# Edge scores of a graph network: rows of 256 columns, added, clipped and weighted, in place of maxima and minima of 257 scaled and sorted columns

## The chip, the cores and the metric

The kernel runs on one core of a Trainium2 chip. The metric is the device time of one execution in microseconds (us); lower is better. Three runs of the kernel before have a median of 3169.38 us, from 3156.57 to 3185.58. Everything is computed in 32-bit floats. The names used here: PE is TensorE (matrix products), DVE is VectorE, ACT is ScalarE, POOL is GpSimd, SP issues transfers.

## The reference, cut to what matters

A batch of 16 graphs with 1024 nodes and 256 features goes through four layers. All share one sparse adjacency matrix `adj` (about 1.6% of it is not zero).

```
# layer 0, for each graph b
pre_u = h @ W1[:256]                      # (1024, 256)
pre_v = h @ W1[256:]                      # (1024, 256)
S[u, v] = sigmoid( sum_k W2[k] * relu(pre_u[u, k] + pre_v[v, k] + b1[k]) + b2 )
a[v]  = sum_u S[u, v] * adj[u, v] * h[u]
m[v]  = (sum_u adj[u, v] * h[u]) * h[v]
z     = beta1*h + beta2*(a @ Wa + ba) + beta3*(m @ Wm + bm)
# layer 1
z     = z + relu((adj @ z) @ W.T + b)
# layers 2 and 3: attention over all pairs of nodes, with adj as a bias in the softmax
```

The change concerns `S`, the edge scores of layer 0. They are needed only where `adj[u, v]` is not zero. `relu(x)` is `max(x, 0)`.

## The kernel before, in words

**Edge lists.** At the start the kernel finds, for each node u, its neighbours v by repeated searches for the eight largest values of a row of `adj` (the loop over `t` in the preparation). The first 16 neighbours of each node go into the lists `slot_v`, the further ones into extra rows of four. 1024 nodes are 8 tiles of 128 nodes (a tile's nodes lie on the 128 partitions); six extra tiles follow. One **edge step** handles one tile and one neighbour slot, for four graphs at once. There are 4 groups of 4 graphs and (8 x 16 + 6 x 4) = 152 steps a group, 608 in all.

**Sides.** `edge_sides` computes for each graph and node the two projected rows and the product with Wa in one go (2 R + 256 columns, copied from PSUM by ScalarE into `st`), and stores them to DRAM as `u_d`, `v_d` and `hw_d`. R is the width of a row: 257 before. Four graphs lie side by side, so a row of a group is 4 R numbers wide.

**The trick with sorted columns.** For a positive weight w, `w * max(a + b, 0)` is `max(w a, -w b) + w b`; for a negative one the maximum becomes a minimum. So the preparation sorts the 256 columns by the sign of W2, scales the u side by W2 and the v side by -W2, and puts the sum of `w b` into one extra column in front. To this end it counts and ranks the signs with many tiny VectorE instructions (from `above` to `to_sign`), turns both halves of W1 by transposes on TensorE, multiplies them with placing matrices (`to_own`, `to_other`), and makes `b1r` and `sign` by products. The columns are cut at fixed places: the first 145 take a maximum (`BIG`, the extra one, 112 surely positive and 32 mixed), the last 112 a minimum, and the 32 mixed ones, where the sign changes, are scaled by their size only and multiplied by their sign afterwards. If the signs do not fit this cut, `uneven` sends the kernel into a slow arm that needs no lists.

**An edge step** (`score_steps`): GpSimd gathers 128 rows of `v_d` by an indirect transfer into one of six tiles z (`fetch`, five steps ahead, lines 1113-1115 through the helper at line 942). The tile u holds the node's own rows: ScalarE copies `b1r` into it (line 1105) and a transfer adds the rows of `u_d` to it (line 1109). Then come three VectorE instructions on z, in place:

```
big, low, mixed = zk[:, :, :BIG], zk[:, :, BIG:], zk[:, :, BIG - MIXED : BIG]
paced(nc.vector.tensor_tensor(big, big, uk[:, :, :BIG], ALU.max))      # line 1076, 4 x 145
paced(nc.vector.tensor_tensor(low, low, uk[:, :, BIG:], ALU.min))      # line 1077, 4 x 112
nc.vector.tensor_tensor(mixed, mixed, sign..., ALU.mult)               # line 1078, 4 x 32
```

One step later four ScalarE passes (line 1031) sum each graph's R columns of z into the score `s`. After a tile's last slot ScalarE applies a tanh, VectorE multiplies by `adj` (line 1036), and GpSimd scatters the values into a dense matrix in DRAM (line 947), from where they come back as `gd`.

**What sets the order.** Beside the edge steps runs the main work: first the products that need no scores (the messages m, the sides of the next graphs; `score_free`), then for each group the products with the dense scores (`with_edges`), layer 1 (`layer_one`, written as seven products of blocks instead of eight, `seven`), and two attention layers (`front`, `sums`). `Side.along` calls one edge step for a fixed amount of main work, by the table `PACE` (0.246 to 0.3 steps per written microsecond of TensorE work). So the 608 steps are interleaved with the main work in program order, on the same engines, and each engine works through its own queue in order. `paced` makes an instruction wait for the sixth TensorE product back in program order. Products are recorded at line 140, whichever function asks for them. In `sums` VectorE makes tiles m (line 1458), three ahead, and four products of TensorE use each. The scores of a group must be finished before its `with_edges`. A scheduler places the instructions of each engine by its own estimate of times, within the dependencies.

Steps and the main work share VectorE with the additions that put the seven products together (`put_together`, line 419), the copies `gc` of the dense scores (line 1490, every second one; the others on ScalarE at line 1492) and the closing additions of each attention layer.

Of the kernel before, what the change touches and what calls it, by code (L numbers as in the profile page):

```python
# [17 lines left out]
P = 128  # L18
# [25 lines left out]
MIXED = 32  # L44
LOW = 3.0e38
# [34 lines left out]
def gnn_stack_kernel(  # L80
# [41 lines left out]
    def bank():  # L122
        return psum[-1].tile([P, HN], F32, tag="bank", name="bank")
# [56 lines left out]
    def column(a, name, queue=nc.gpsimd):  # L180

        t = const.tile([P, DH], F32, name=name)
        queue.dma_start(t, a.rearrange("(h p) -> p h", p=P))
        return t
# [5 lines left out]

    SURE = (D - MIXED) // 2
    BIG = 1 + SURE + MIXED
    R = 1 + D
    b1r = const.tile([P, R], F32, name="b1r")
    sign = const.tile([P, MIXED], F32, name="sign")
# [307 lines left out]
    with ExitStack() as stack:  # L503
# [5 lines left out]
        def first_group():  # L509
# [13 lines left out]
        index = prep1.tile([P, DH], F32, name="index")  # L523
        nc.gpsimd.iota(
            index, pattern=[[P, DH]], base=0, channel_multiplier=1, allow_small_or_imprecise_dtypes=True
        )
        places = prep1.tile([P, D], F32, name="places")
        nc.gpsimd.iota(
            places, pattern=[[1, D]], base=0, channel_multiplier=0, allow_small_or_imprecise_dtypes=True
        )  # L530

        w2c = column(g0_W2.rearrange("d o -> (d o)"), "w2c", nc.sync)
        b1c = column(g0_b1, "b1c", nc.scalar)
# [9 lines left out]
        def tiny(name):  # L543
            return prep1.tile([P, DH], F32, name=name)

        above = tiny("above")
        nc.vector.tensor_scalar(above, w2c, 0.0, None, ALU.is_gt)
        counted = bank()
        nc.tensor.matmul(counted[:, :DH], below, above, start=True, stop=True)
        nc.tensor.matmul(counted[:, DH : 2 * DH], ones, above, start=True, stop=True)  # L550
        work = first_group()
        next(work)
        rank, n_above = tiny("rank"), prep1.tile([P, DH], F32, name="n_above")
        nc.vector.tensor_copy(n_above, counted[:, DH : 2 * DH])
        nc.vector.tensor_copy(rank, counted[:, :DH])
        nc.vector.tensor_scalar(rank[:, 1:], rank[:, 1:], n_above[:, 0:1], None, ALU.add)
        n_all = prep1.tile([P, 1], F32, name="n_all")
        nc.vector.tensor_tensor(n_all, n_above[:, 0:1], n_above[:, 1:2], ALU.add)
        others, place = tiny("others"), tiny("place")
        nc.vector.tensor_tensor(others, index, rank, ALU.subtract)  # L560
        nc.vector.scalar_tensor_tensor(others, others, n_all, rank, ALU.add, ALU.subtract)
        nc.vector.tensor_tensor(place, others, above, ALU.mult)
        nc.vector.tensor_tensor(place, others, place, ALU.subtract)
        nc.vector.tensor_tensor(place, place, rank, ALU.add)
        size, scale, back = tiny("size"), tiny("scale"), tiny("back")
        nc.vector.scalar_tensor_tensor(size, w2c, -1.0, w2c, ALU.mult, ALU.max)
        nc.vector.tensor_scalar(scale, place, float(SURE + MIXED), None, ALU.is_lt)
        nc.vector.tensor_tensor(size, size, w2c, ALU.subtract)
        nc.vector.tensor_tensor(size, size, scale, ALU.mult)
        nc.vector.tensor_tensor(scale, size, w2c, ALU.add)  # L570
        nc.vector.tensor_scalar(back, scale, -1.0, None, ALU.mult)
        signs = tiny("signs")
        nc.vector.tensor_scalar(signs, above, 2.0, -1.0, ALU.mult, ALU.add)
        to_own = prep1.tile([P, DH, R], F32, name="to_own")
        to_other = prep1.tile([P, DH, R], F32, name="to_other")
        to_sign = prep1.tile([P, DH, MIXED], F32, name="to_sign")
        nc.vector.memset(to_own[:, :, 0], 0.0)
        nc.vector.tensor_copy(to_other[:, :, 0], w2c)
        for kh in range(DH):
            for dst, by, at in (  # L580
                (to_own[:, kh, 1:], scale, slice(0, D)), (to_other[:, kh, 1:], back, slice(0, D)),
            ):
                placed = nc.vector.tensor_scalar(
                    dst, places[:, at], place[:, kh : kh + 1], by[:, kh : kh + 1], ALU.is_equal, ALU.mult
                )
        for kh in range(DH):
            late = nc.vector.tensor_scalar(
                to_sign[:, kh, :], places[:, SURE : SURE + MIXED], place[:, kh : kh + 1], signs[:, kh : kh + 1],
                ALU.is_equal, ALU.mult,
            )  # L590
            after(tc, late, [placed], mybir.DependencyClass.NoSync, "behind the weights")
        w1 = prep1.tile([P, DH, 2 * R + D], F32, name="w1p")
        turned_w = {}
        for side in range(2):
            ps = bank()
            for kh in range(DH):
                for dh in range(DH):
                    at = (kh * DH + dh) * P
                    nc.tensor.transpose(ps[:, at : at + P], raw[:, dh, side, kh * P : (kh + 1) * P], ident)
            turned_w[side] = prep1.tile([P, DH, DH * P], F32, name=f"turned_w{side}")  # L600
            nc.scalar.activation(turned_w[side], ps.rearrange("p (k d) -> p k d", k=DH), AF.Copy)
        for side, to_side in ((0, to_own), (1, to_other)):
            for dh in range(DH):
                ps = bank()
                for kh in range(DH):
                    nc.tensor.matmul(
                        ps[:, :R], turned_w[side][:, kh, dh * P : (dh + 1) * P], to_side[:, kh, :],
                        start=kh == 0, stop=kh == DH - 1,
                    )
                nc.scalar.activation(w1[:, dh, side * R : (side + 1) * R], ps[:, :R], AF.Copy)  # L610
        last_w = nc.vector.tensor_scalar(w1[:, :, 2 * R :], raw[:, :, 2, :], beta2, 0.5, ALU.mult, ALU.mult)
        nc.sync.dma_start(w_d, w1.rearrange("p c k -> p (c k)"))
        ps = bank()
        for kh in range(DH):
            nc.tensor.matmul(
                ps[:, :R], b1c[:, kh : kh + 1].to_broadcast([P, P]), to_own[:, kh, :],
                start=kh == 0, stop=kh == DH - 1,
            )
        nc.scalar.activation(b1r, ps[:, :R], AF.Copy)
        nc.vector.memset(b1r[:, 0:1], -LOW)  # L620
        ps = bank()
        for kh in range(DH):
            nc.tensor.matmul(ps[:, :MIXED], ones, to_sign[:, kh, :], start=kh == 0, stop=kh == DH - 1)
        nc.vector.tensor_copy(sign, ps[:, :MIXED])

        spare_row = prep1.tile([P, NF], F32, name="spare_row")
# [1403 lines left out]
```

## Time and profile before

One execution was profiled: 3179.84 us, of which 3178.1 us are the span from the first instruction to the last.

| what | busy us | share of the span |
|---|---|---|
| TensorE (PE) | 3034.1 | 95% |
| VectorE (DVE) | 2077.4 | 65% |
| ScalarE (ACT) | 1815.8 | 57% |
| GpSimd (POOL) | 1679.1 | 53% |

| group of instructions | count | mean ns |
|---|---|---|
| line 1031, ScalarE pass that sums 257 columns | 2432 | 410 |
| line 1031, reading its accumulator | 2432 | 193 |
| line 942, gather of 128 rows of 4 x 257 | 512 | 1139 |
| line 947, scatter of scores | 512 | 1118 |
| line 1458, tile m of the attention sums | 512 | 745 |

How to read it: busy times of an engine count each moment once, while the mean of a group is that of single instructions, which may overlap by some tens of ns at their ends. A row of groups gives the line, the engine, the operation, what is written and read, partitions x elements, the count, the busy time of the group with the mean of one, and the idle time of the engine just before them with what ended most of it. A line of waits reads "who <- whom: us in total, times, longest". In a matrix product, each of the two records counts as one instruction.

### The profile page before, as it was taken

The numbers are of one execution on the slowest core, as the hardware profiler recorded it, in microseconds if no ns is written. First come the engines' busy times: TensorE is split into PE (matmuls) and PEld (weight loads), VectorE is DVE, ScalarE is ACT, GpSimd is POOL, SyncE is SP. The second block draws the span as 40 slices with busy tenths as digits, with TensorE's granted clock in tenths as the row PEclk, the third lists the DMA queues.
The fourth block names the chain that finished last, engine by engine and source line by source line (L and its number), as shares of the span: only waits on it lengthen the run. The fifth ranks groups of instructions, "written<-read, shape, count | busy, mean of one in ns | idle before, by whom it ended". The sixth has DMA issues, their size and how long they took to land. (4 is left out here: it accounts for less than half of the span.)

```text
span 3178.1 us, 40600 instructions
## 1 busy us (share of the span) xinstructions
PE 3034.1 (95%) x11774; PEld 2158.6 (68%) x11774; DVE 2077.4 (65%) x4093; ACT 1815.8 (57%) x6461; POOL 1679.1 (53%) x1481
## 2 busy tenths in 40 slices
PE   8899999899998999999999899999999999989999
PEld 5445444444546855887785588878658888858888
DVE  8857565656574676777666677766767763258844
ACT  3326565566674866777676577867757762213342
POOL 1116566777563576555667764656665550077600
PEclk9999999999999999999999999999999999999999
DMA  8978997988999987558988755788875555485600
GB/s 290 321 281 294 311 286 244 299 258 238 287 266 338 309 261 240 149 157 248 304 272 260 228 159 154 244 302 279 271 224 160 155 162 169 146 273 167 165 7 28
DMA packets 314738, 731.46 MB, mean 230 GB/s; under 512 B 50493, under 2 KB 144762, under 8 KB 307338
## 3 DMA queue, kind: packets, MB, share of 16 engines
q0 software_dynamic: 128064, 388.90, 41.7%
q1 hardware_dynamic: 148234, 271.98, 26.0%
q10 hardware_dynamic: 38208, 67.91, 5.8%
q8 instruction: 95, 1.56, 0.2%
q14 instruction: 137, 1.12, 0.1%
HBM read 592.10 MB, written 136.53 MB: 229 GB/s over the span
## 5 line engine op out<-in xcount | busy, mean ns | idle before, releaser
L1031 ACT ACTIVATE z<-z 128x257 f32<-128x257 f32 x2432 | 985.1, 410 | 569.4 <-DVE z L1078 303.3
L140 PE MATMUL bank<-feats,m 128*128 128x257 f32 x4096 | 925.1, 384 | 26.8 <-DVE m L1458 15.6
L140 PEld LDWEIGHTS bank<-feats,m 128*128 128x128 f32 x4096 | 775.3, 192 | 147.6 <-DVE m L1458 17.9
L942 POOL DMA_INDIRECT z<-v_d,slot_v x512 | 583.1, 1139 | 541.8 <-ACT z L1031 278.8
L1076 DVE TENSOR_TENSOR z<-z,u 128x580 f32<-128x580 f32 x608 | 461.7, 759 | 427.1 <-PE bank L140 185.1
L947 POOL DMA_INDIRECT dense_d<-gt,slot_at x512 | 572.2, 1118 | 187.9 <-issue 142.0
L140 PE MATMUL bank<-gc,hw 128*128 128x256 f32 x2048 | 454.1, 383 | 27.5 <-ACT gc L1492 17.6
L1031 ACT ACTIVATION_READ_ACCUMULATOR z<-z 128x1 f32 x2432 | 468.3, 193 | 2.1 <-issue 2.1
L1458 DVE SCALAR_TENSOR_TENSOR m<-rho,tau,adj_sb 128x512 f32<-128x512 f32 x512 | 374.8, 745 | 140.4 <-PE bank L140 120.8
L140 PEld LDWEIGHTS bank<-gc,hw 128*128 128x128 f32 x2048 | 388.3, 191 | 92.8 <-ACT gc L1492 24.0
L1077 DVE TENSOR_TENSOR z<-z,u 128x448 f32<-128x448 f32 x608 | 375.8, 618 | 0.0
L140 PE MATMUL bank<-w1p,hT 128*128 128x385 f32 x1024 | 346.1, 491 | 11.7 <-issue 5.3
L140 PEld LDWEIGHTS bank<-w1p,hT 128*128 128x128 f32 x1024 | 193.8, 190 | 162.7 <-issue 30.1
L140 PE MATMUL bank<-g_wT,z 128*128 128x257 f32 x1024 | 233.4, 382 | 5.7 <-DVE t L419 2.7
L140 PE MATMUL bank<-adj_sb,h 128*128 128x512 f32 x504 | 224.6, 595 | 0.0
L140 PEld LDWEIGHTS bank<-g_wT,z 128*128 128x128 f32 x1024 | 192.8, 191 | 38.1 <-issue 4.7
L1492 ACT ACTIVATE gc<-gd 128x1024 f32<-128x1024 f32 x64 | 132.1, 2064 | 124.3 <-PE bank L140 93.3
L942 POOL DMA_INDIRECT z<-v_d,x_node x96 | 129.0, 1343 | 137.4 <-ACT z L1031 67.1
L369 ACT ACTIVATE st<-bank 128x385 f32<-128x385 f32 x256 | 121.6, 483 | 132.2 <-PE bank L140 78.9
L140 PEld LDWEIGHTS bank<-adj_sb,h 128*128 128x128 f32 x504 | 96.1, 191 | 115.9 <-issue 107.4
L1078 DVE TENSOR_TENSOR z<-z,sign 128x128 f32<-128x128 f32 x608 | 172.6, 284 | 0.0
L140 PE MATMUL bank<-adjT_in,t 128*128 128x512 f32 x352 | 155.2, 593 | 4.0 <-DMA adjT_in<-sumT_d 3.7
(248 smaller groups left out, 3245.7 us busy)
## 6 DMA issues: line engine op xcount, KB each, us to landing
gd<-dense_d SPq DMA_DIRECT2D x128, 512.0 KB
dense_d<-zero ACTq DMA_DIRECT2D x64, 512.0 KB
h<-in_x_dram SPq DMA_DIRECT2D x19, 1024.0 KB
u_d<-st SPq DMA_DIRECT2D x128, 128.5 KB
v_d<-st SPq DMA_DIRECT2D x128, 128.5 KB
u<-u_d POOLq DMA_DIRECT2D x32, 514.0 KB
hw_d<-st SPq DMA_DIRECT2D x128, 128.0 KB
zb_d<-zb ACTq DMA_DIRECT2D x16, 1024.0 KB
```

Of the source, the lines that this page charges most:

```text
L140: recent.append(nc.tensor.matmul(*args, **kw))
L369: nc.scalar.activation(st[:, cols], ps[:, :half], AF.Copy)
L942: return nc.gpsimd.indirect_dma_start(out=dst, out_offset=None, in_=src[:], in_offset=bass.IndirectOffsetOnAxis(ap=at, axis=0), **how,)
L947: return nc.gpsimd.indirect_dma_start(out=dst[:], out_offset=bass.IndirectOffsetOnAxis(ap=at, axis=0), in_=src, in_offset=None,)
L1031: nc.scalar.activation(zk[:, c, :], zk[:, c, :], AF.Copy, accum_out=s[:, k, c : c + 1])
L1076: paced(nc.vector.tensor_tensor(big, big, uk[:, :, :BIG], ALU.max))
L1077: paced(nc.vector.tensor_tensor(low, low, uk[:, :, BIG:], ALU.min))
L1078: nc.vector.tensor_tensor(mixed, mixed, sign[:, None, :].to_broadcast([P, GB, MIXED]), ALU.mult)
L1458: nc.vector.scalar_tensor_tensor(m, r[:, cols], ta[:, kt : kt + 1], ea[:, kt, cols], ALU.max, ALU.mult)
L1492: paced(nc.scalar.activation(gc, by_batch, AF.Copy), 16)
```

## The change

Rows are 256 columns wide. Neither side is scaled or sorted; there is no extra column, no sign, no cut. `b1r` and a new constant `w2r` are `b1` and `W2` themselves, read from DRAM into all partitions. A step adds u to z over all 4 x 256 numbers, and a second instruction takes the maximum with 0 and multiplies by `w2r`, which is repeated for the four graphs. The preparation uses W1 as it was loaded; only Wa is scaled by beta2 / 2 in place. Loads of `w2c` and `b1c`, which only the slow arm needs now, move from the SP and ScalarE queues to GpSimd's. Three waits ("behind the weights") that held back instructions of the preparation go, and so does the test `uneven`.

```diff
-    SURE = (D - MIXED) // 2
-    BIG = 1 + SURE + MIXED
-    R = 1 + D
-    b1r = const.tile([P, R], F32, name="b1r")
-    sign = const.tile([P, MIXED], F32, name="sign")
+    R = D
+    b1r = everywhere(g0_b1, D, "b1r")
+    w2r = everywhere(g0_W2.rearrange("d o -> (d o)"), D, "w2r")
...
-        w2c = column(g0_W2.rearrange("d o -> (d o)"), "w2c", nc.sync)
-        b1c = column(g0_b1, "b1c", nc.scalar)
+        w2c = column(g0_W2.rearrange("d o -> (d o)"), "w2c")
+        b1c = column(g0_b1, "b1c")
...
-        above = tiny("above")
-        nc.vector.tensor_scalar(above, w2c, 0.0, None, ALU.is_gt)
-        counted = bank()
-        nc.tensor.matmul(counted[:, :DH], below, above, start=True, stop=True)
...
+        w1 = raw.rearrange("p c s k -> p c (s k)")
+        nc.vector.tensor_scalar(w1[:, :, 2 * R :], w1[:, :, 2 * R :], beta2, 0.5, ALU.mult, ALU.mult)
+        nc.sync.dma_start(w_d, w1.rearrange("p c k -> p (c k)"))
         work = first_group()
         next(work)
...
-        w1 = prep1.tile([P, DH, 2 * R + D], F32, name="w1p")
-        turned_w = {}
-        for side in range(2):
-            ps = bank()
-            for kh in range(DH):
-                for dh in range(DH):
-                    at = (kh * DH + dh) * P
-                    nc.tensor.transpose(ps[:, at : at + P], raw[:, dh, side, kh * P : (kh + 1) * P], ident)
...
-        last_w = nc.vector.tensor_scalar(w1[:, :, 2 * R :], raw[:, :, 2, :], beta2, 0.5, ALU.mult, ALU.mult)
-        nc.sync.dma_start(w_d, w1.rearrange("p c k -> p (c k)"))
...
-            first = nc.vector.tensor_scalar(
+            nc.vector.tensor_scalar(
                 left, row, 0.0, 0.0, ALU.not_equal, ALU.add, accum_out=there[:, t : t + 1]
             )
-            after(tc, first, [placed], mybir.DependencyClass.NoSync, "behind the weights")
...
-                    zk, uk = z.rearrange("p (c k) -> p c k", k=R), u.rearrange("p (c k) -> p c k", k=R)
-                    big, low, mixed = zk[:, :, :BIG], zk[:, :, BIG:], zk[:, :, BIG - MIXED : BIG]
-                    paced(nc.vector.tensor_tensor(big, big, uk[:, :, :BIG], ALU.max))
-                    paced(nc.vector.tensor_tensor(low, low, uk[:, :, BIG:], ALU.min))
-                    nc.vector.tensor_tensor(
-                        mixed, mixed, sign[:, None, :].to_broadcast([P, GB, MIXED]), ALU.mult
+                    zk = z.rearrange("p (c k) -> p c k", k=R)
+                    paced(nc.vector.tensor_tensor(z, z, u, ALU.add))
+                    nc.vector.scalar_tensor_tensor(
+                        zk, zk, 0.0, w2r[:, None, :].to_broadcast([P, GB, R]), ALU.max, ALU.mult
                     )
```

## The prediction

> **What bounds the kernel now.** I read the page's busy shares first, then its slices, then windows by stage, then the groups of VectorE, then who waits for whom.
>
> From the page, busy time and slices:
>
> ```profile
> PE 3034.1 (95%) x11774; PEld 2158.6 (68%) x11774; DVE 2077.4 (65%) x4093; ACT 1815.8 (57%) x6461; POOL 1679.1 (53%) x1481
> ...
> PE   8899999899998999999999899999999999989999
> ...
> DVE  8857565656574676777666677766767763258844
> ```
>
> TensorE is busy 95% of the span in nearly every slice: it bounds the kernel. VectorE has a third of its time free on average, but from slice 14 to slice 33 of 40 it stands at six to seven tenths. The last 570 us hold no edge step.
>
> The groups of the page for the changed lines (out<-in, shape, count | busy us, mean ns | idle before):
>
> ```profile
> L1076 DVE TENSOR_TENSOR z<-z,u 128x580 f32<-128x580 f32 x608 | 461.7, 759 | 427.1 <-PE bank L140 185.1
> ...
> L1077 DVE TENSOR_TENSOR z<-z,u 128x448 f32<-128x448 f32 x608 | 375.8, 618 | 0.0
> ...
> L1078 DVE TENSOR_TENSOR z<-z,sign 128x128 f32<-128x128 f32 x608 | 172.6, 284 | 0.0
> ```
>
> There are 608 edge steps, each with these three instructions. Their spans overlap, so the queue's cost comes from the timeline of VectorE (start us, length us):
>
> ```profile
> 1337.44 0.76 DVE L1076 TENSOR_TENSOR z<-z,u 128x580 f32<-128x580 f32 x1
> 1338.11 0.62 DVE L1077 TENSOR_TENSOR z<-z,u 128x448 f32<-128x448 f32 x1
> 1338.65 0.29 DVE L1078 TENSOR_TENSOR z<-z,sign 128x128 f32<-128x128 f32 x1
> 1338.85 0.75 DVE L1458 SCALAR_TENSOR_TENSOR m<-rho,tau,adj_sb 128x512 f32<-128x512 f32 x1
> ```
>
> From the start of the first to the start of what follows is 1338.85 - 1337.44 = 1.41 us: this is what a step costs VectorE's queue now.
>
> Where the steps run, by windows of 100 us (PE, PEld, DVE, ACT, POOL busy, with counts; then clock, DMA share, GB/s), all instructions first and line 1076 alone after:
>
> ```profile
> 600.00:700.00 100.00, 95.23 (x255) 47.95 (x254) 64.06 (x121) 61.72 (x252) 70.38 (x64) 0.97 0.84 259
> 1300.00:1400.00 100.00, 100.00 (x487) 87.50 (x487) 77.30 (x170) 81.42 (x299) 65.14 (x54) 1.00 0.56 155
> 1700.00:1800.00 100.00, 100.00 (x307) 57.16 (x307) 73.74 (x143) 64.30 (x265) 76.12 (x59) 1.00 0.81 260
> ```
>
> ```profile
> 600.00:700.00 100.00, 20.48 (x27) 0.97 0.84 259
> 1300.00:1400.00 100.00, 19.02 (x25) 1.00 0.56 155
> 1700.00:1800.00 100.00, 21.17 (x28) 1.00 0.81 260
> ```
>
> TensorE has nothing to give in these windows, VectorE 23 to 36 us, and 25 to 28 steps fall in each. That is the number the change must fit into: about 1 us more per step.
>
> **The change, part by part.**
>
> *The step on VectorE.* Out go three instructions over 580 + 448 + 128 = 1156 numbers of a partition, in come two over 1024 each. Two-input f32 work here runs at one speed: (759 - 618) / (580 - 448) = 1.07 ns a number, with 139 ns beside it. An add of 1024 stands in the trace (groups by shape), and so does a scalar_tensor_tensor with a plain constant, at half the length:
>
> ```profile
> L1194 DVE TENSOR_TENSOR sums<-adj_sb 128x1024 f32<-128x1024 f32 x2 | 2.4, 1224 | 3.9 <-PE bank L140 3.9
> L1642 DVE SCALAR_TENSOR_TENSOR z<-y,z 128x512 f32<-128x512 f32 x28 | 19.2, 687 | 0.1
> ```
>
> The add costs 1.22. The second is 687 ns + 512 x 1.07 = 1.23 us. Its repeated row w2r should cost nothing extra: line 978, with an operand repeated over a stride of zero, takes 279 ns for 128 numbers, like line 1078 (284). The second reads what the first writes, so they don't overlap: a dependent pair in the trace (line 419, then 462) starts 0.72 us apart at a length of 0.68, so + 0.04. Successors overlap by about 0.08 (1338.85 against 1338.65 + 0.29). The slot is 1.22 + 0.04 + 1.23 - 0.08 = 2.41 us, taken as 2.40, against 1.41: **+0.99 us a step, +602 us over 608 steps**. Below, the two could overlap as 1076 and 1077 do: 2.26 us, +0.85. Above, the second could run like line 1458 (745 ns for 512 numbers, 58 ns more): +1.06.
>
> The Trainium skill, "VectorE: DVE Perf Modes", section "Rules for kernel authors", says to minimise the count of operations. By that rule alone, three becoming two, the step would fall to two thirds of 1.41 us, a gain of 286 us of VectorE's time hidden under TensorE, and the kernel would stay where it is; the rows above go by numbers moved, 2048 against 1156, so I follow the rows.
>
> *How much of 602 us lies beside TensorE.* The issue order of the changed program keeps TensorE's order of main work the same, and sets each step's place in VectorE's queue within six instructions of where it was. So the load can be laid over the old windows: to VectorE's busy time add 0.99 / 0.759 = 1.30 us for each us of line 1076, and what exceeds the window is late. Summed over the run this gives 9 us in windows of 100 us, 27 in 50, 107 in 20, 192 in 10. The window to take is how long TensorE goes on without VectorE. In the stretches of attention sums (about 1200-1600, 1800-2100, 2300-2600 us) that is three tiles m made ahead; one tile feeds four products, each two records of 925.1 / 4096 = 0.226 us, so 3 x 1.81 = 5.4 us. There I take 10 us: **+80 us** (20 us: 51). Elsewhere the banks are the cover: two of eight are filled in a block of the seven products, whose four steps have a written cost of 1.72 us each, so about three blocks or 20 us of lag are allowed. There I take 20 us: **+56 us** (10 us: 112). Together +136 us. With +0.85 and +1.06 the same choice gives 60 + 39 = 99 and 91 + 66 = 157.
>
> What waits behind a late step: in VectorE's queue the tiles m, the adds that free banks, every second copy gc; on ScalarE four accumulating passes, which already wait for VectorE:
>
> ```profile
> ACT z L1031 <- DVE z L1078: 303.3, 153, 9.7
> POOL z L942 <- ACT z L1031: 346.0, 157, 12.5
> PE bank L140 <- DVE m L1458: 15.6, 12, 2.3
> ```
>
> The last row is today's direct price, 15.6 us. The first two are covered by five gathers fetched ahead; if that cover goes, ScalarE's evacuations come late too (rival C).
>
> The gathers' issue on GpSimd doesn't lengthen with VectorE's load: 1108 ns from 120 to 1000 us, 1123 from 1300 to 1480, where VectorE is busier.
>
> *Rows of 256 columns.* ScalarE passes lose one column of 257 (1.5 ns of 410), products 384 of 385 columns: nothing. Gathered rows shrink from 4112 to 4096 bytes, 0.4%.
>
> The Trainium skill, "DMA: Bandwidth & Descriptors", section "How a descriptor splits into AXI transactions", says that a transfer not starting at a multiple of 256 bytes pays for bytes it doesn't use. By it a row of 4112 at such a pitch takes 17 transactions and one of 4096 takes 16 (an estimate from that page); no row of this trace shows it, and it speaks for the change.
>
> *The start.* Out go the sorting (about 30 tiny VectorE instructions between 4 and 10 us, while VectorE waits for adj until 16.21 anyway) and TensorE's 12.08 to 19.6 us of weight turning. But in the new issue order VectorE scales Wa only as its fourth instruction, behind two counting passes and a maximum over adj, so at 16.2 + 3 x 1.13 = 19.6, done near 20.1, and the third product of the first tile waits for it; products started at 20.18 before, with a stop until 24.51 that goes. That is about 1.5 us. The end of the start is VectorE's chain from 16.2 to 106.8 us, unchanged but for under 1 us, and three small products and 3 us of VectorE after it. **-2 us** (0 to -7, the whole of the weight turning).
>
> *Sum.* Against the profiled execution, 3179.84 us: + 136 - 2 = 3314. That execution was 10 us above the median of the runs, 3169.38; on the median it is 3303, given as **3300 us**.
>
> **The rivals.**
>
> A, the forecast: VectorE binds locally. For: VectorE plus the addition passes 20 us in 45 of 159 windows of 20 us. Its own bounds are +99 to +157 and one finer window either way, 3240 to 3365.
>
> B, the cover holds: TensorE tolerates 50 us of lag. For: over 100 us only 4 of 32 windows overflow. 3169 + 27 - 2 = 3194, from 3165 to 3215. Against: only three tiles m are made ahead.
>
> C, the lag spreads through ScalarE: the four passes wait on VectorE in ScalarE's queue with evacuations of feats and st behind them. Priced as 10 us windows everywhere with +1.06: 217 us, 3384; with half of today's 303 us of such waits repeated on the path beyond A, 3450. For: ScalarE is 81% busy from 1300 to 1400.
>
> D, faster: the aligned rows relieve the DMA. Place: 115 to 1000 us, where the DMA share is 0.90 and TensorE idles 60 us. Price: if all of that goes, 3169 - 60 - 2 = 3107. It decides only if VectorE fits there with less than 28 us of overflow: 548.9 + 212 x 0.99 = 759 of 885 us fits on average, but 20 us windows say that about 40 us don't. Against: TensorE's waits in that stretch name VectorE and ScalarE more than DMA.
>
> That the change doesn't do what it says (an instruction that runs at two numbers per ns) has no row: every two-input f32 instruction shows 1.05 to 1.09 ns.
>
> **How the numbers follow.** A 0.63, C 0.16, B 0.16, D 0.05. A measurement of this kernel tells about 1% from no change (runs 3156.57 to 3185.58). Slower by over 1% (above 3201): A, C and a third of B, 0.84; within: 0.11 from B; faster: 0.05 from D. The range goes from inside B, 3185, to inside C, 3410; that leaves out D, half of B and a third of C, 0.18.
>
> **What would show it.** Two groups of 608 replace three, near 1220 and 1230 ns, VectorE busy near 2680 us. PE waits for m and for z rise far above 15.6 us, most between 1200 and 2600. The last 570 us keep their length. The first product runs before 20 us but the barrier comes at 109 instead of 111. I am wrong if the scalar_tensor_tensor takes other than about 1.23 us, if TensorE's wait on VectorE stays small while VectorE passes 90%, or if the stretch up to 1000 us gets shorter.

## The result, and the profile after

The changed kernel took **3197.57 us** (median of 12 runs, 3191.94 to 3205.7) against 3167.07 us for the kernel before, measured in turn with it (12 runs, 3156.57 to 3185.58): a ratio of **1.0099, 95% interval [1.0079, 1.0118]**. It is slower by 30 us, where 3300 us, 131 us more than the median before, had been forecast. The profiled execution took 3198.51 us, its span 3196.8 us.

Busy shares and slices of the page of the changed kernel:

```profile
PE 3032.8 (95%) x11738; PEld 2157.9 (68%) x11738; DVE 2569.7 (80%) x3455; ACT 1822.2 (57%) x6454; POOL 2008.3 (63%) x1483
...
PE   7899999997998999999999999999999999999999
...
DVE  7868888877986887999988899988889983257844
```

VectorE's busy time rose from 2077.4 to 2569.7 us, by 492 us or 0.81 us a step, and stands at nine tenths in nine of slices 17 to 32. TensorE's busy time is what it was. GpSimd's rose too, by 329 us, which nothing in the forecast provided for.

The two groups that replace lines 1076 to 1078 (busy us, mean ns of one, idle before):

```profile
L978 DVE TENSOR_TENSOR z<-z,u 128x1024 f32<-128x1024 f32 x608 | 738.0, 1217 | 225.5 <-DMA z<-v_d,slot_v 94.9
...
L979 DVE SCALAR_TENSOR_TENSOR z<-z,w2r 128x1024 f32<-128x1024 f32 x608 | 736.8, 1218 | 5.2
```

Their lengths are the forecast ones. Their place is not: the scheduler put other work between the two. VectorE's timeline in the attention sums (start us, length us):

```profile
1336.20 1.21 DVE L979 SCALAR_TENSOR_TENSOR z<-z,w2r 128x1024 f32<-128x1024 f32 x1
1337.34 0.29 DVE L1639 RECIPROCAL share<-bank 128x1 f32<-128x1 f32 x3
1337.55 0.72 DVE L1359 SCALAR_TENSOR_TENSOR m<-rho,tau,adj_sb 128x512 f32<-128x512 f32 x1
1338.20 1.21 DVE L978 TENSOR_TENSOR z<-z,u 128x1024 f32<-128x1024 f32 x1
1339.33 0.74 DVE L1359 SCALAR_TENSOR_TENSOR m<-rho,tau,adj_sb 128x512 f32<-128x512 f32 x1
1339.99 1.21 DVE L979 SCALAR_TENSOR_TENSOR z<-z,w2r 128x1024 f32<-128x1024 f32 x1
1341.13 0.27 DVE L1306 TENSOR_REDUCE shift<-tops 128x1 f32<-128x128 f32 x1
```

Here an add takes 1339.33 - 1338.20 = 1.13 us of the queue and the second instruction 1.14, and the step does not pay for the dependence between them. That holds for 408 of the 608 steps; in the other 200 the second instruction follows the add at once and starts 1.23 us behind it on average, so these pay about 0.09 us.

The same three windows of 100 us, counted from the start of this span (PE, PEld, DVE, ACT, POOL busy, with counts; clock, DMA share, GB/s):

```profile
600.00:700.00 100.00, 93.19 (x248) 46.28 (x247) 83.02 (x91) 58.14 (x237) 80.93 (x63) 0.97 0.79 249
1300.00:1400.00 100.00, 100.00 (x488) 87.36 (x487) 98.64 (x151) 78.45 (x294) 74.32 (x55) 1.00 0.56 162
1700.00:1800.00 100.00, 93.51 (x266) 51.35 (x265) 82.98 (x97) 61.52 (x240) 80.55 (x49) 0.97 0.76 243
```

In the attention sums (1300 to 1400) VectorE is 98.6% busy, and TensorE has still lost nothing. In the other two, where VectorE has 17 us to spare on average, TensorE idles almost 7. What TensorE waits for, over the whole span (us in total, times, longest):

```profile
PE bank L138 <- DVE t L415: 17.5, 6, 6.0
PE bank L138 <- ACT mT L461: 15.6, 4, 6.9
PE bank L138 <- DVE z L1543: 12.1, 4, 3.8
PE bank L138 <- DVE gc L1391: 9.0, 8, 1.3
...
PE bank L138 <- DVE m L1359: 3.5, 3, 1.7
```

These are the sums that put the seven products together (line 415), an evacuation on ScalarE (461), layer 1's ending (1543) and copies (1391). The tiles m, from which the largest loss had been expected, cost 3.5 us, less than the 15.6 before.

### The profile page after: what moved, and what is told of

Its sections match the earlier page's. It is cut to its first block, busy times and chain, and to the rows that moved or that the text cites. A ratio compares the mean times of both kernels' runs of the same rounds, so it can differ in the third digit from the quotient of the medians.

```text
span 3196.8 us, 39491 instructions
## 1 busy us (share of the span) xinstructions
PE 3032.8 (95%) x11738; PEld 2157.9 (68%) x11738; DVE 2569.7 (80%) x3455; ACT 1822.2 (57%) x6454; POOL 2008.3 (63%) x1483
## 5 line engine op out<-in xcount | busy, mean ns | idle before, releaser
L934 ACT ACTIVATE z<-z 128x256 f32<-128x256 f32 x2432 | 983.3, 408 | 691.4 <-DVE z L979 583.3
L978 DVE TENSOR_TENSOR z<-z,u 128x1024 f32<-128x1024 f32 x608 | 738.0, 1217 | 225.5 <-DMA z<-v_d,slot_v 94.9
L845 POOL DMA_INDIRECT z<-v_d,slot_v x512 | 703.8, 1375 | 333.1 <-ACT z L934 141.8
L850 POOL DMA_INDIRECT dense_d<-gt,slot_at x512 | 712.1, 1391 | 185.2 <-issue 139.9
L979 DVE SCALAR_TENSOR_TENSOR z<-z,w2r 128x1024 f32<-128x1024 f32 x608 | 736.8, 1218 | 5.2
L138 PE MATMUL bank<-w1p,hT 128*128 128x384 f32 x768 | 261.1, 492 | 11.4 <-DVE mT L415 5.8
L138 PEld LDWEIGHTS bank<-w1p,hT 128*128 128x128 f32 x768 | 146.7, 192 | 128.2 <-issue 22.6
L138 PE MATMUL bank<-sums,t 128*128 128x512 f32 x312 | 156.5, 649 | 28.5 <-ACT mT L461 15.6
L845 POOL DMA_INDIRECT z<-v_d,x_node x96 | 146.7, 1528 | 48.7 <-issue 18.3
L365 ACT ACTIVATE st<-bank 128x384 f32<-128x384 f32 x256 | 118.8, 478 | 81.4 <-PE bank L138 64.1
```

The lines of the kernel that those rows point to most:

```text
L138: recent.append(nc.tensor.matmul(*args, **kw))
L365: nc.scalar.activation(st[:, cols], ps[:, :half], AF.Copy)
L845: return nc.gpsimd.indirect_dma_start(out=dst, out_offset=None, in_=src[:], in_offset=bass.IndirectOffsetOnAxis(ap=at, axis=0), **how,)
L850: return nc.gpsimd.indirect_dma_start(out=dst[:], out_offset=bass.IndirectOffsetOnAxis(ap=at, axis=0), in_=src, in_offset=None,)
L934: nc.scalar.activation(zk[:, c, :], zk[:, c, :], AF.Copy, accum_out=s[:, k, c : c + 1])
L978: paced(nc.vector.tensor_tensor(z, z, u, ALU.add))
```

## The experiments

**The same two kernels on a later occasion.** Unedited, the kernel before (c1) and the changed one (c2, c4) ran again, to see whether 30 us is what the change costs. c1 and c2 ran on chip 4, c4 on chip 9, each beside runs of the kernel before.

> The kernel before, unchanged, for its profile beside the other runs: the kernel before took 3167.07 us (median of 12) when it was compared with the changed kernel, but 3079.0 us (median of 13) beside the runs of the first experiments. If the level belongs to the chip or to the occasion, this run shows what TensorE waits less for; then the changed kernel beside it shows whether it gains as much (theory: same ratio, about 1.01) or not (rival: it stays near 3195 us, ratio 1.035 to 1.04, as the forecast of +134 us had it).

> The changed kernel, unchanged, in the same call as the kernel before. Theory C (the two levels of the kernel before are a matter of the chip, and both kernels share them): 3079 x 1.0099 = 3110 us. Rival (the changed kernel is bound by VectorE's load, which no faster chip relieves): 3185 to 3205 us, 3.5 to 4% slower than the kernel before in the same call.

> The changed kernel a third time. On the first occasion it took 3197.57 us against 3167.07 of the kernel before, later 3190.35 against 3077.41. Theory (the kernel before varies by occasion, the changed one hardly): the changed kernel lands between 3185 and 3200, and the kernel before at either 3077 or 3167; the ratio is 1.038 or 1.010 with nothing between that the changed kernel explains. Rival (both move together): the changed kernel moves by as much as the kernel before does.

Measured: the kernel before 3076.33 us, 0.9999 [0.9987, 1.001] of its own runs beside it (3077.41); the changed one 3190.35, **1.0383 [1.0359, 1.0407]**, and 3198.04, 1.0397 [1.0379, 1.0415] of 3077.48. So both times the change cost **113 to 121 us**, and what differs from the first result is the kernel before: 90 us faster than it was. The changed kernel stayed within 8 us of 3197.57. The files are the same, and so is the order of VectorE's instructions in the two traces of the kernel before. The chip of the first comparison is not known, so whether the 90 us belong to a chip or to a moment can't be told; the later runs on two chips agree (3077.41 and 3077.48 us).

Busy shares of c1 and c2:

```profile
PE 2997.6 (98%) x11774; PEld 2150.7 (70%) x11774; DVE 2088.1 (68%) x4093; ACT 1821.1 (59%) x6461; POOL 1665.8 (54%) x1481
```

```profile
PE 3027.5 (95%) x11738; PEld 2157.4 (68%) x11738; DVE 2570.6 (81%) x3455; ACT 1821.9 (57%) x6454; POOL 2015.5 (63%) x1483
```

The slower execution of the kernel before had idle time on its engines for which the profile shows no cause. Waits named "issue" (ended by nothing that the profile shows) and "remote" (ended by a queue that it doesn't name) in the first profile of the kernel before, then in c1:

```profile
ACT z L1031 <- issue: 199.9, 90, 11.0
DVE z L1076 <- issue: 79.5, 36, 11.9
...
DVE z L1076 <- remote: 32.1, 9, 10.5
PE bank L140 <- issue: 24.5, 23, 2.5
```

```profile
ACT z L1031 <- issue: 124.6, 64, 7.6
DVE z L1076 <- issue: 15.8, 13, 2.1
```

At the step's line VectorE idled 79.5 + 32.1 - 15.8 = 96 us more without a cause, and c1 has no row of "issue" or "remote" for TensorE's products at line 140. The changed kernel had some of this on the first occasion too, far less on VectorE. Its first profile, then c2:

```profile
ACT z L934 <- issue: 91.6, 42, 8.6
DVE z L978 <- issue: 25.3, 12, 6.8
```

```profile
DVE z L978 <- issue: 2.3, 2, 1.7
...
ACT z L934 <- issue: 0.8, 3, 0.3
```

Where the time goes is seen by subtracting the moments at which the same points of the program are reached (us; worked out from the traces, difference to c1):

```
point of the program (its time in c1)             before, first   changed, first     c2
lists found, first group's sides made (111)            + 0.2           + 2.9       +  3.7
sides of all groups made (899)                         +42.0           +59.3       + 66.1
first group: copies of its scores made (1055)          +37.7           +61.6       + 65.6
  layer 1 done, attention sums begun (1234)            +45.0           +84.3       + 86.4
  attention sums done (1475)                           +55.2           +80.8       + 84.6
second group: copies made (1594)                       +57.6           +78.8       + 81.9
  attention sums begun (1772)                          +69.7          +100.0       +101.8
  attention sums done (2013)                           +86.0           +98.4       +100.2
third group: copies made (2126)                        +84.5          +100.2       +104.9
  attention sums begun (2304)                          +92.2          +119.0       +121.1
  attention sums done (2545)                          +101.5          +117.5       +120.1
end (3063)                                            +109.1          +127.6       +120.3
```

Against c1, c2 loses 62 us while the sides are made and 21, 20 and 16 us between the copies and the sums of three groups, where layer 1 is. **In the three stretches of attention sums it loses nothing**, nor after the last edge steps. The first execution of the kernel before lost some of its time in every stage, 36 us of it in the attention sums.

**How much VectorE work a step can carry.** e1 leaves out the second instruction: the maximum with 0 and the multiplication by `w2r` are not done. e10 does it on two of the four graphs only. e2 and e3 add a maximum of z with itself, over half a row or all of it, which changes no value.

```diff
  e1_add_only
-                    nc.vector.scalar_tensor_tensor(zk, zk, 0.0, w2r..., ALU.max, ALU.mult)
  e10_half_second
+                    nc.vector.scalar_tensor_tensor(zk[:, :2, :], zk[:, :2, :], 0.0, w2r..., ALU.max, ALU.mult)
  e2_half_more (behind the second instruction)
+                    nc.vector.tensor_tensor(zk[:, :2, :], zk[:, :2, :], zk[:, :2, :], ALU.max)
  e3_full_more
+                    nc.vector.tensor_tensor(z, z, z, ALU.max)
```

> The changed kernel without its second instruction: the maximum with 0 and the multiplication by w2r are left out, so the scores are sums of u + v + b1 alone. A step costs VectorE about 1.14 us instead of 2.27 (before: 1.41); everything else of the change stays (rows of 256, the new start). Theory V (VectorE's load makes the whole loss): back to the time before or under it, 3150 to 3170 us, the waits of TensorE for additions gone. Rival S (the loss comes from the start, the rows or the transfers): stays at 3185 to 3200 us. GpSimd's gathers: near 1150 ns if their lengthening comes from VectorE's two-input work, near 1375 ns if it comes from the rows.

> The changed kernel with its second instruction over half of the row, 512 of 1024 numbers: the maximum with 0 and the multiplication by w2 are left out for the other two of four edges. A step then costs VectorE's queue about 1.72 us, 0.3 more than before. Theory (TensorE goes on for about 10 us without VectorE; windows of 10 us give 9 to 27 us of lateness at 0.31 more per step): 3077 + 10 to 30 = 3087 to 3107, a ratio of 1.003 to 1.010. Rival (cover of 50 us or more): nothing, 3077. Rival (loss in proportion to VectorE's added time, 113 us for 0.81): 113 x 0.31 / 0.81 = 43 us, 3120.

> The changed kernel with a third instruction in each step, a maximum of the first 512 of the 1024 numbers with themselves (about 0.6 us, values unchanged). VectorE's busy time would be about 2570 + 608 x 0.6 = 2935 us. Theory V with a cover of 5 to 10 us as in the prediction: 3169 + 250 to 355 = 3420 to 3525 us (windows of 20 and 10 us with 1.4 us more per step). Theory V with a cover of about 50 us: 3169 + 143 = 3312 us. Rival S: 3200 to 3215 us.

> The changed kernel with a third instruction over all 1024 numbers (about 1.14 us). VectorE's busy time would be about 2570 + 608 x 1.14 = 3260 us, above the span: it must bind. Theory V with a short cover: 3169 + 509 to 618 = 3680 to 3790 us; with a cover of 50 us or more: 3169 + 390 to 418 = 3560 to 3590 us. Rival S: less than 3400 us is impossible even for it, since about 690 us without steps stand beside 608 steps of 3.4 us and VectorE's other work.

Busy shares of e1, e10, e2 and e3:

```profile
PE 2991.4 (97%) x11738; PEld 2145.8 (70%) x11738; DVE 1926.3 (63%) x2847; ACT 1819.8 (59%) x6454; POOL 1798.6 (59%) x1483
```

```profile
PE 2996.5 (97%) x11738; PEld 2148.9 (70%) x11738; DVE 2282.9 (74%) x3455; ACT 1832.0 (59%) x6454; POOL 1827.6 (59%) x1483
```

```profile
PE 3112.0 (90%) x11738; PEld 2185.3 (63%) x11738; DVE 2925.6 (84%) x4063; ACT 1856.6 (54%) x6454; POOL 2161.9 (62%) x1483
```

```profile
PE 3178.4 (85%) x11738; PEld 2214.9 (59%) x11738; DVE 3241.7 (87%) x4063; ACT 1836.7 (49%) x6454; POOL 2398.4 (64%) x1483
```

"VectorE per step" is the difference of its busy time to c1's 2088.1 over 608. TensorE's idle time is summed from its records (c1: 60.5 us). The last two columns apply the forecast's window method to c1's own trace.

```
run   time us   ratio, interval            VectorE per step   TensorE idle   TensorE busy   lateness in 10 us / 20 us windows
e1    3076.94   0.9997 [0.9982, 1.0012]    -0.27              +  6.7         -  6.2              -
e10   3093.46   1.0057 [1.0034, 1.0079]    +0.32              + 20.7         -  1.1          10 /   0
c2    3190.35   1.0383 [1.0359, 1.0407]    +0.79              + 90.6         + 29.9          99 /  42
e2    3463.43   1.1242 [1.1198, 1.1287]    +1.38              +279.4         +114.4         321 / 245
e3    3748.78   1.2186 [1.2161, 1.221]     +1.90              +497.8         +180.8         587 / 526
```

Two things follow. Everything else in the change (rows of 256, no sorting, no weights turned), together with 0.27 us less VectorE work a step, comes to nothing over the whole run: e1 stands at 0.9997. It isn't nothing in each stage: in the traces e1 is 11 us behind c1 when the sides of all groups are made, and has regained them by the third group's copies. And the loss comes with the second instruction's work on VectorE, beginning at about 0.3 us more a step and growing faster than in proportion, as the windows say. TensorE's idle time in c2 is in sum that of windows of 10 us, not of 20 (e10 has twice the 10 us windows, and at the two largest loads the measured idle time falls between the two windows or below).

The sum agrees partly by luck. For c2's +0.79 the windows of 10 us give 34 us where the sides are made, 20 in the layer-1 stretches of three groups and 35 in the attention sums; TensorE's idle time beyond c1's is 50, 31 and 2 us there. At e2's load the stages agree better (windows 104, 69 and 118 us; idle time 89, 64 and 95): there the attention sums do lose.

**Where VectorE was when TensorE waited.** In the layer-1 stretches VectorE is busy in nearly all of the 10 us before TensorE's waits. Between 120 and 1000 us, where the sides are made, it is another matter: VectorE is 81% busy there, and in the 10 us before c2's 21 waits of TensorE above 1 us, and during them, it is 70% busy. Behind 16 of these 21 waits (59 of 70 us) VectorE had stood idle for over 1 us for a transfer, mostly the gather of a tile z; a moment taken at random has that behind it in 36% of cases. (After 1000 us it is 5 of 20 waits, with VectorE 91% busy around them.) Such stops are not new: c1 has 28 of them there, 115 us together, and c2 27, 118 us. New is that TensorE waits behind them, 21 times for 70 us against 7 times for 35. That a fuller VectorE no longer catches up after a stop fits this and is argued, not shown; nor is it ruled out that later gathers, whose issue takes longer (last section), add to it. VectorE's waits for gathers over the whole span, c1, then c2:

```profile
DVE z L1076 <- DMA z<-v_d,slot_v: 62.1, 33, 7.0
```

```profile
DVE z L978 <- DMA z<-v_d,slot_v: 116.8, 58, 8.0
```

The time lost is more than the idle time: from c2 to e3 TensorE's busy time grows by a third to two fifths of it. c2 shows why, in TensorE's timeline at one such wait:

```profile
788.76 3.60 PE L138 MATMUL bank<-mT,wm 128*128 128x512 f32 x8
800.62 5.27 PE L138 MATMUL bank<-sums,t 128*128 128x512 f32 x8 [8.26 <-ACT mT L461]
```

and in windows (the clock is the third number from the end):

```profile
780.00:790.00 10.00, 8.39 (x31) 4.37 (x30) 4.46 (x5) 6.75 (x26) 8.18 (x8) 1.00 0.77 197
...
800.00:805.00 5.00, 4.38 (x7) 2.02 (x8) 4.96 (x7) 4.36 (x19) 3.88 (x4) 0.62 0.89 184
805.00:810.00 5.00, 5.00 (x13) 2.15 (x12) 5.00 (x6) 3.85 (x17) 4.39 (x3) 1.00 0.47 132
```

Eight products of one shape took 3.60 us before the wait of 8.26 us and 5.27 after it, at a granted clock of 0.62. So this wait cost 8.26 + 1.67 us. The same place shows a path by which TensorE comes to wait through ScalarE. ScalarE's timeline of c2, then VectorE's:

```profile
796.07 0.42 ACT L934 ACTIVATE z<-z 128x256 f32<-128x256 f32 x1 [8.21 <-DVE z L979]
...
799.58 0.42 ACT L934 ACTIVATE z<-z 128x256 f32<-128x256 f32 x1 [1.79 <-DVE z L979]
799.90 0.19 ACT L934 ACTIVATION_READ_ACCUMULATOR z<-z 128x1 f32 x1
799.99 0.58 ACT L461 ACTIVATE mT<-bank 128x512 f32<-128x512 f32 x1
```

```profile
793.55 1.23 DVE L978 TENSOR_TENSOR z<-z,u 128x1024 f32<-128x1024 f32 x1 [9.09 <-DMA u<-u_d]
```

The evacuation of mT, for which TensorE waits, stands in ScalarE's queue behind two steps' passes that wait for VectorE's second instruction. But VectorE's load did not start this wait: it had stood idle for 9.09 us until the transfer of the node's own rows (u) landed, at the first step of the second group. At the same step of c1 VectorE idles 7.92 us for the same transfer, and TensorE waits 3.66 us behind it.

**What the cover is.** e4 asks for the tiles m of the attention sums one ahead instead of three, in the changed kernel; e6 orders each tile m behind the whole step, so that none comes between its two instructions.

```diff
  e4_after_ahead1
-AHEAD = 3
+AHEAD = 1
  e6_m_behind_step
+                    weighted[:] = [second]          # the step's second instruction
...
+                        after(tc, made_m, weighted, mybir.DependencyClass.NoSync, "behind the whole step")
```

> The changed kernel with one tile m made ahead in place of three. Theory (three tiles of 1.81 us are the cover that hides VectorE's lag in the attention sums): TensorE waits for m in most of the 512 tiles, 0.3 to 0.8 us each, the time rises by 100 to 300 us over the changed kernel in this call. Rival (the cover lies elsewhere, in the mean load): less than 30 us.

> The changed kernel with one rule more for the order: a tile m goes behind the whole step that was issued before it, so no m stands between the two instructions of a step (141 of 512 did). Theory O (the small loss is owed to the order, which lets m in after one instruction of 1.13 us): m waits up to 2.3 us more and each pair without anything between pays about 0.1 us for its dependence; TensorE's waits for m rise from 3.5 us to 15 to 40 us and the time to 3215 to 3240 us. Rival (three tiles m in advance cover a whole step anyway): 3195 to 3205 us, waits for m under 10 us.

Measured: e4 3191.59 us, 1.038 [1.0357, 1.0402], the same as c2. e6 3207.61, 1.043 [1.0402, 1.0459], 10 to 17 us more than c2 and c4. e4 doesn't settle what covers VectorE in the attention sums, for the scheduler left the tiles m where they were: from the end of a tile m to the first product that uses it, the median over the first three groups is 3.65 us in e4 and 3.66 in c2 (4.36 in c1). In e6 it is 2.37 us, and from the first product to the last of the attention sums of these groups e6 loses 24 us against c1 where c2 loses 5.5 and e4 12; in e2 it is 1.79 us and the loss 141. So the less lead the tiles m have, the more these sums lose, which speaks for the forecast's cover; no run varied that lead alone.

**The start.** e7 puts the scaling of Wa first in VectorE's queue.

```diff
+            after(tc, first, [scaled_w], mybir.DependencyClass.NoSync, "behind the scaling of Wa")
...
+                after(tc, top, [scaled_w], mybir.DependencyClass.NoSync, "behind the scaling of Wa")
```

> The changed kernel with the scaling of Wa ahead of the counting passes and maxima over adj in VectorE's queue. TensorE's wait of 8.3 us for it at 15 us goes; products of the first graphs run 5 to 8 us earlier. Theory: the end of the start is set by VectorE's chain over adj, so the barrier at about 113.5 us moves by 0 to -2 us and the time by as much. Rival: the start is set by the products, and the time falls by 5 to 8 us.

Measured: 3197.64 us, 1.0396 [1.0362, 1.0431], no different from c2 and c4. The wait of TensorE for this scaling (8.3 us in the first profile of the changed kernel, 9.7 in c2) is not on the path that sets the end of the start: VectorE is done with the lists at 115.6 us in e7 and at 115.5 in c2.

**Does a late VectorE absorb pauses?** The first result would follow if a changed kernel that waits for VectorE anyway hid the idle time that cost the kernel before 90 us. e8 and e9 give ScalarE 854 small copies of a scratch, in the kernel before and the changed one; e11 and e12 give VectorE one long maximum after every 33rd step.

```diff
  e8_before_pauses, e9_after_pauses (behind the step's instructions)
+                    [nc.scalar.activation(idle, idle, AF.Copy) for _ in range(14 if n % 10 == 5 else 0)]
  e11_before_vector_pauses, e12_after_vector_pauses
+                    n % 33 == 16 and nc.vector.tensor_reduce(idle, z[:, None, :1024].to_broadcast([P, 8, 1024]), AX.X, ALU.max)
```

> The kernel before, with 14 small copies of a scratch of 128 numbers on ScalarE after every tenth edge step: 61 pauses of about 4 us, 250 us of ScalarE in all, about as much as ScalarE's idle time without a visible cause in the first profile of the kernel before. Theory (such pauses are what the first occasion cost the kernel before): 30 to 100 us more than 3077, so 3107 to 3177. Rival (ScalarE has 41% to spare and hides them): within 10 us of 3077, and then the pauses of the first profile must have cost through VectorE, whose own were 109 us.

> The same pauses in the changed kernel, to be read against the run with pauses in the kernel before. Theory (a kernel whose VectorE is late anyway absorbs them): 0 to 25 us more than 3190, so 3190 to 3215, and the ratio of the two with pauses falls from 1.038 towards 1.01 to 1.025. Rival (the pauses add up with the late steps): as much more as the kernel before gains, 30 to 100 us, so 3220 to 3290 and a ratio that stays near 1.038.

> The kernel before, with one long maximum over the finished tile z (8 times 1024 numbers, about 8.5 us) on VectorE after every 33rd edge step: 18 pauses, about 150 us of VectorE in all, about as much as VectorE's idle time without a visible cause in the first profile of the kernel before had over the later one. Theory (such pauses cost the kernel before most of their length, since TensorE goes on for only about 10 us without VectorE): 40 to 110 us more than 3077, so 3117 to 3187, like the first occasion's 3167. Rival (TensorE's lead covers 8.5 us): within 15 us of 3077.

> The same 18 long pauses of VectorE in the changed kernel. Theory (the changed kernel, late on VectorE already, absorbs pauses): at most half of what the kernel before gains, 0 to 50 us above 3195. Rival (pauses on the engine that is late add up in full): more than the kernel before gains, 60 to 150 us, 3255 to 3345; then the ratio of 1.010 on the first occasion is not made by absorbing, and the changed kernel must have had fewer such pauses, as its profile shows (35 us on VectorE against 109).

Measured: e8 3105.87 us (1.0093 [1.0075, 1.0112]), 28 us more than the kernel before; e9 3207.82 (1.0415 [1.0393, 1.0436]), 10 to 17 more than the changed kernel. The scheduler did not leave the copies in place but spread them over some 200 stretches before 1135 us, nearly all under 4 us, so this pair is a weak test; as far as it goes, the changed kernel pays less for copies on ScalarE than the kernel before. The VectorE pair stayed whole. e11's group of VectorE:

```profile
L1081 DVE TENSOR_REDUCE idle<-z 128x8 f32<-128x8192 f32 x18 | 156.2, 8680 | 0.2
```

e11 took 3132.02 us (1.0183 [1.0162, 1.0204]), 56 more than the kernel before for 156 us of pauses. e12 took 3340.96 (1.0867 [1.0841, 1.0893]), **143 to 151 more than the changed kernel**. The changed kernel absorbs no pauses of VectorE: it pays for them almost in full, the kernel before for a third. For VectorE that explanation of the first result falls. For ScalarE it stays open: the changed kernel's first profile has 73 us more of ScalarE's stalls above 2 us than c2 (last section), at nearly the same time. What remains for VectorE is that the changed kernel had fewer such pauses on VectorE (25.3 us before its add, against 111.6 before line 1076). Why it had fewer, and where they come from, stays open. They do not account for everything either: 96 us at e11's price of 56 / 156 are 34 us (an estimate), not 90. ScalarE's stalls, 134 us more in the first profile of the kernel before than in c1, would add 13 at e8's price of 28 us for 288 us of copies.

## Why the prediction was wrong, and where it was right

**The step that failed is the base of the sum**, "Against the profiled execution, 3179.84 us: + 136 - 2 = 3314". It took all of that execution's time as the kernel's own and put the lateness on top. But the same file takes 3077 us on another occasion, where the changed kernel takes 3190 to 3198, hardly other than 3197.57. So the loss did not come on top of 3169, but on top of some 3077. On 3077 the same sum gives 3211, 13 to 21 us too much. The profile had the sign of it: "issue" was TensorE's longest row of waits for products (24.5 us), ahead of "DVE m" (15.6), which the forecast showed alone as "today's direct price" (c1 has neither row); and TensorE idled 133 us between its first and last product, of which c1 has 60.5. That the base varied is shown. That the changed kernel was spared on the occasion when the kernel before was not is measured, and its reason is not known. So the forecast was wrong about the ratio there by four times (1.0099 against 1.041), and near it on the later occasions (1.038 to 1.040).

**The step's price.** The two instructions were right to 1%: 1217 and 1218 ns for 1220 and 1230. The slot was too long: 2.27 us, or 2.36 where the pair stands back to back, and 2.30 on average, not 2.40. VectorE's busy time rose by 0.81 us a step, not 0.99. The forecast let every pair stand back to back; in two of three steps other instructions lie between.

**The cover.** The method (windows, and 10 to 20 us of lead) gave the sum within a factor of two for loads from 0.3 to 1.9 us a step. Its division by stage was wrong. The attention sums, given windows of 10 us and +80, lost nothing in c2, and TensorE's waits for m fell to 3.5 us instead of rising far above 15.6: there VectorE passed 90% and TensorE did not wait, which the forecast itself had named as a sign of being wrong. The rest, given 20 us and +56, lost all 120; the forecast's own figure for 10 us there was 112. Three blocks of lag by the banks was too much: what is late are the sums of the seven products, layer 1's endings and evacuations, directly on VectorE or behind ScalarE's passes. And the windows know only VectorE's load; behind most waits where the sides are made stands a transfer that VectorE waited for. The path through ScalarE is rival C's; but only some 40 us of TensorE's waits in c2 name ScalarE, against 25 in c1.

**A term that was missing** is the clock: of c2's 120 us, 90.6 are idle time and 29.9 slower products after it. It was made up for by the step's price, which was too high. The agreement of 113 to 121 us with the forecast 134 owes something to that.

**Rival B** gave 3194 us, which is nearly what was measured first, by a cover of 50 us. That was luck, as its mechanism is refuted: by it c2 would have cost some 7 us.

**Rows of 256 columns** neither cost nor gained anything that shows in the time, as forecast (e1: 0.9997, with 0.27 us less VectorE work a step), so rival D and the 17 transactions of the rule on alignment have no weight that could be seen here. The weighing of "minimise the count of operations" against the rows went the right way: 3 to 2 operations, and 492 us more of VectorE.

**The start** was forecast at -2 us and came out +2.7 (first profiles; +3.7 in c2): adj arrived at 19.63 us instead of 16.21. That the last 570 us keep their length was right within 2.5 us on the first occasion and 0.2 on the later one.

**"The gathers' issue on GpSimd doesn't lengthen with VectorE's load"** was wrong; see the last section.

## What to carry to other kernels

A forecast "time before + what is added" is only as good as the time before: look first for idle time of the bounding engine without a cause, and forecast against the time without it. Lay a new load over the trace in windows as short as the lead of the bound engine, some 10 us here, stage by stage, and count the slower clock after each wait. Look also for the stops that the loaded engine makes for transfers: with less free time it may not catch up after them. And ask for each stage what the bound engine takes from the loaded one: the stage with the highest load (98.6%) lost nothing here, and those at 81 to 89% (the making of the sides, layer 1) lost nearly all. Last, before an edit's result is read, see in the trace whether the edit moved what it was to move: one of these did not.

## What the runs showed of the hardware that was not expected

**Indirect transfers are issued more slowly under two-input instructions of VectorE.** The gathers' groups, of the kernel before and of the changed one:

```profile
L942 POOL DMA_INDIRECT z<-v_d,slot_v x512 | 583.1, 1139 | 541.8 <-ACT z L1031 278.8
```

```profile
L845 POOL DMA_INDIRECT z<-v_d,slot_v x512 | 703.8, 1375 | 333.1 <-ACT z L934 141.8
```

Of c2's 1216 gathers of z and scatters of scores, 863 had two-input instructions of VectorE, with both inputs in SBUF, beside them for at least half of their first 600 ns: 1533 ns on average. The 174 that had none there took 1059 ns (median 979). The mean of the gathers from slot_v rises with VectorE's load a step: 1147 ns in c1, 1270 in e10, 1374 in c2, 1532 in e2, 1776 in e3. Without the second instruction it is 1233 (e1), so the rows of 256, which e1 has too, are not the main cause. The Trainium skill, "SBUF — State Buffer", section "SBUF: two separate sides", says that a VectorE instruction with two inputs in SBUF and a GpSimd instruction that reads SBUF lock each other out of a shared pair of ports for a whole instruction. The numbers agree with it. In c1, with three instructions of 580, 448 and 128 numbers, the same sorting gives 1195 and 1022 ns. GpSimd's busy time grew by 350 us from c1 to c2; no run here separates what that cost.

**A pause costs TensorE more than its length**: c2 to e3 show 0.33 to 0.41 us of slower products for each us of additional idle time. The Trainium skill, "TensorE: Matmul & The Clock Gate", section "Why this matters for your kernels", warns of idle gaps above about 3 us between products; the 8.26 us gap with the clock at 0.62 behind it agrees.

**The same program took 3167 and 3077 us on two occasions**. Between 120 and 2650 us the first profile has 74 stalls above 2 us of ScalarE and VectorE that no record explains, 347 us in all, and c1 has 24, 86 us; for the changed kernel it is 25 (107 us) and, in c2, 2 (6 us). The durations of single instructions do not differ (line 1031: 410 and 409 ns; line 1076: 759 and 760). Nothing points to the loading of the program: 18 of the 74 have a packet of the two instruction queues in them, where a third of stretches of these lengths would have one at random. The cause was not found.
